# Image 0 of a convolution-and-attention kernel: its start in a written order, a place of its own for the rows of each unit, both halves' angles at once, image 1's statistics moved

## The chip, the cores and the metric

The kernel runs on one core of a Trainium2 chip. The core has five engines with queues of their own: PE (TensorE, matrix multiplication), DVE (VectorE), ACT (ScalarE), POOL (GpSimd) and SP (SyncE, which here issues every DMA). The metric is the device time of one execution in microseconds (us); shorter is better. All data is float32. PE writes to PSUM, which this kernel uses as six banks of 128 x 512 for general use and two for accumulators; everything else on the chip lies in SBUF, 128 partitions wide.

## What is computed

The input `x` is a batch of 16 images of 256 channels and 64 x 64 pixels. Two layers follow each other, each of the form x = x + layer(groupnorm(x)), where the group norm has 32 groups of 8 channels.

```python
# layer 0
pooled = x.mean(axis=(2, 3))
h = relu(pooled @ ap_w1.T + ap_b1)
angles = tanh(h @ ap_w2.T + ap_b2) * (pi / 4)
rot = vmap(vmap(_rotate_one))(base_kernel, angles)     # bilinear rotation of 3x3 kernels
out = conv(x, rot)                                      # 8 groups of 32 channels, own kernels per image
mod = sigmoid(relu(pooled @ meta_w1.T + meta_b1) @ meta_w2.T + meta_b2)
x = x + out * mod
# layer 1
q = xt @ Wq.T + bq;  k, v = split(xt @ Wkv.T + bkv)
scale = softplus(scale_param)
q, k = focused(relu(q) / scale), focused(relu(k) / scale)   # cubed, length kept
z = 1 / (q . k.sum + 1e-6)
out = q @ (k^T v) * z + depthwise5x5(v)
x = x + (out @ Wproj.T + bproj)
```

The statistics of the first norm need the whole image, so in each image the order is forced: statistics, angles and modulation, rotated kernels, convolution (with the residual folded in as an identity in the kernel's centre), statistics of the second norm, keys and values for all pixels, then queries and output.

## The kernel before

**Tiles.** An image is cut into 8 chunks (`NCH`) of 512 pixels; 256 channels are two halves of 128 partitions. `load_stats` loads a chunk into a buffer of the pool `xin` (12 buffers, tag "x"), `take_stats` has DVE take its statistics (`bn_stats`, one for each half). The convolution takes two chunks at a time, a **unit** `u` of four quarters `q` (a chunk and a half each); `load_rows` brings a unit's pixels, with one row above and one below, to 32 partitions per quarter in four DMAs. Where the row lies outside the image it is filled with the channel's mean (`edge`), by POOL.

**Preparation of an image.** `prepare(b)` is a generator; each `yield` ends a piece. In turn: group norm coefficients, the two small networks, tanh and sines, the `edge` values, then for each half `weights(t)` (angles to bilinear weights `mix`), `products` (POOL multiplies the base kernel by three of the nine mixes), `reduce` (DVE sums nine products), `finish`, `spread` (ACT copies the rotated kernels into the layout `wt` that PE reads), and `shifts` (48 small matmuls for both halves that give the bias which stands for the subtracted mean). For image 0 all pieces are written one after the other. For later images one piece is taken in each half of a `key_step` of the image before: for image 1 in the steps 4 to 15 of image 0, two pieces a step; what is left is taken in front of `between`. From image 2 on three pieces come earlier, at the end of the attention of the image before that.

**Convolution.** `convolve(b, u)` issues the unit's matmuls, 32 x 32 tiles on 16 places of PE at once, into four of the six PSUM banks. The first 16 products need all four quarters and all four `j` of `wt`. `evict` (ACT) moves a bank to SBUF and adds `shift`, `settle` (DVE) corrects the edge columns and takes the statistics of the second norm.

**Image 0.** Its units' rows go to two buffers in turn (`rows_of`: `xr`, and part of the tile `fm` that the attention uses later), so units 2 and 3 are loaded when the convolutions of units 0 and 1 have read theirs. Then `norm1(0)` gives the coefficients of the second norm, and the keys follow, 16 steps of 256 pixels. In the steps 0 to 3 the statistics of image 1 are taken, two chunks a step; `load_kernels(1)` and `prepare(1)` start at step 4.

**Order.** From the statement `with tc.manual_schedule()` in front of the image loop on, each engine works in the order in which the program is written. Everything in front of it (statistics of image 0, `prepare(0)`, the constants, the softplus of the scale and the scaling of `Wq` and `Wkv` by it, the zeros around `vpad`, four units of convolution) is ordered by a planner that may exchange independent instructions. Constants for the attention (`wp`, `band`, `dwb`, ...) are loaded by SP behind the first rows. `vh` holds the values in the layout of the 5 x 5 depthwise convolution; POOL sets it to zero once, and its margin columns stay zero for the whole run.

Of the kernel before, what the change touches and what calls it, by code (L numbers as in the profile page):

```python
# [15 lines left out]
P = 128  # L16
# [34 lines left out]
def conv_attention(ctx: ExitStack, tc: tile.TileContext, x, consts, kw, b1, w2, b2, b2r,  # L51
# [55 lines left out]

    for i in range(NCH):
        load_stats(0, i)
        take_stats(0, i)  # L110
# [21 lines left out]

    xbuf = [const("xr", [P, 4, CROWS])]
    xbuf.append(fmp.tile([P, 16, C], F32, tag="fm", name="xr_first").rearrange("p T n -> p (T n)")
                [:, 0:4 * CROWS].rearrange("p (g n) -> p g n", g=4))

    def rows_of(b, u):
        return xbuf[u % 2 if b == 0 else 0]
# [44 lines left out]
    def prepare(b):  # L183
# [5 lines left out]
        for t in range(2):  # L189
            nc.vector.tensor_scalar(gm[:, t, :], gmask, mean[:, t:t + 1], None, ALU.mult)  # L190
# [36 lines left out]
        state[b]["edge"] = edge  # L227
        nc.vector.tensor_scalar(mod, mod, 0.5, 0.5, ALU.mult, ALU.add)
# [8 lines left out]
        def weights(t):  # L237


            u = rotp.tile([P, 18], F32, tag="u", name=f"u_{b}_{t}")  # L240
            nc.vector.tensor_scalar(u, cgrid, cs[:, 0, t:t + 1], None, ALU.mult)
            nc.vector.scalar_tensor_tensor(u, sgrid, cs[:, 1, t:t + 1], u, ALU.mult, ALU.add)
            hat = rotp.tile([P, 3, 18], F32, tag="hat", name=f"hat_{b}_{t}")
            nc.vector.tensor_scalar(hat[:, 0, :], u, -1.0, 0.0, ALU.mult, ALU.max)
            nc.vector.tensor_scalar(hat[:, 2, :], u, 0.0, None, ALU.max)
            nc.vector.tensor_add(u, hat[:, 0, :], hat[:, 2, :])
            nc.vector.tensor_scalar(hat[:, 1, :], u, -1.0, 1.0, ALU.mult, ALU.add)
            yield
            mix = rotp.tile([P, 9, 9], F32, tag="mix", name=f"mix_{b}_{t}", bufs=2)
            hx = hat[:, :, 0:9].rearrange("p k n -> p n k")  # L250
            hy = hat[:, :, 9:18].rearrange("p k n -> p n k")
            nc.vector.tensor_scalar(hat[:, :, 9:18], hat[:, :, 9:18], a[:, t:t + 1], None, ALU.mult)
            nc.vector.tensor_mul(
                mix.rearrange("p n (y x) -> p n y x", y=3),
                hy.unsqueeze(3).to_broadcast([P, 9, 3, 3]),
                hx.unsqueeze(2).to_broadcast([P, 9, 3, 3]),
            )
            base = kw_t[:, ts(t, KB)].rearrange("p (o q) -> p o q", q=9)
            nc.gpsimd.tensor_mul(base, base, mod[:, t].unsqueeze(2).to_broadcast([P, HD, 9]))
            rots.append(rotp.tile([P, 9, HD], F32, tag="rotw", name=f"rot_{b}_{t}", bufs=2))  # L260
            mixes.append(mix)
            bases.append(base)
# [9 lines left out]

        def reduce(t, n, tmp):
            nc.vector.tensor_reduce(rots[t][:, 3 * n:3 * n + 3], tmp, AX.X, ALU.add)

        def finish(t):
            rs = rotp.tile([P, 3, HD], F32, tag="rsum", name=f"rsum_{b}_{t}")
            nc.vector.tensor_reduce(rs, rots[t].rearrange("p (r x) o -> p x o r", x=3), AX.X, ALU.add)
            sums.append(rs)

            nc.gpsimd.tensor_add(rots[t][:, 4], rots[t][:, 4], sel[:, 0:HD])
# [18 lines left out]
        yield from weights(0)  # L300
        yield
        for t in range(2):
            for n in range(3):
# [5 lines left out]
                if n == 0 and t == 0:  # L309
                    yield from weights(1)  # L310
# [5 lines left out]
                if t == 1 and n == 1:  # L316
                    shifts(0)
        for j in range(4):
            spread(1, (j,))
            yield  # L320
        shifts(1)

    def load_rows(b, u):


        for q in range(4):
            i, t = 2 * u + q // 2, q % 2
            src = x[b, ts(t, P)].rearrange("(g c) n -> c g n", g=4)
            lo, hi = CH * i - W, CH * (i + 1) + W
            d = rows_of(b, u)[ts(q, HD)]  # L330
            mean = state[b]["edge"][ts(q, HD), ts(t, 4)].unsqueeze(2).to_broadcast([HD, 4, W])
            if lo < 0:
                nc.gpsimd.tensor_copy(d[:, :, 0:W], mean)
                nc.sync.dma_start(d[:, :, W:CROWS], src[:, :, 0:hi])
            elif hi > N:
                nc.gpsimd.tensor_copy(d[:, :, CROWS - W:CROWS], mean)
                nc.sync.dma_start(d[:, :, 0:CROWS - W], src[:, :, lo:N])
            else:
                nc.sync.dma_start(d, src[:, :, lo:hi])
# [42 lines left out]
    for _ in prepare(0):  # L382
        pass
    for u in range(2):
        load_rows(0, u)

    wp_t = const("wp", [P, 2, C], halves(wp))
    bp_t = const("bp", [P, 2], bp)  # L390
    dwb_t = const("dwb", [P, 2], dwb)
    band_t = const("band", [KP, HD, BR * BC], band)
# [4 lines left out]
    for name, src, bsrc in (("kv", wkv, brow[C:3 * C]), ("q", wq, brow[0:C])):  # L397
# [6 lines left out]
    inv_t, sa, se, su = (  # L404
        wsp.tile([P, C], F32, tag=k, name=f"soft{n}") for n, k in enumerate(("wkv", "wq", "bkv", "bq"))
    )
    sw = rp.tile([P, C], F32, tag="r1", name="soft4")
    nc.sync.dma_start(inv_t, srow.partition_broadcast(P))


    nc.scalar.activation(sa, inv_t, AF.Abs)
    nc.scalar.activation(se, sa, AF.Exp, scale=-1.0)
    nc.vector.tensor_scalar(su, se, 1.0, None, ALU.add)
    nc.scalar.activation(sa, su, AF.Ln)
# [18 lines left out]

    pb = bank("pb")[:, 0:2]
    for co in range(2):
        for t in range(2):
            nc.tensor.matmul(pb[:, co:co + 1], lhsT=wp_t[:, t, ts(co, P)], rhs=dwb_t[:, t:t + 1],
                             start=t == 0, stop=t == 1)
    nc.vector.tensor_add(bp_t, bp_t, pb)


    vpad = [dcp.tile([BC, H + 4, NJ, C], F32, tag=f"vpad{n}", name=f"vpad{n}") for n in range(2)]
    zt = xp.tile([BC * NJ, 2, C], F32, tag="x", name="zero")
    nc.gpsimd.memset(zt, 0.0)
    for v in vpad:
        for k in range(BC):
            for y in (0, H + 2):
                nc.sync.dma_start(v[k, y:y + 2].rearrange("y j n -> j y n"), zt[0:NJ])


    vh = const("vh", [KP, NR // 2, NJ, C])
    nc.gpsimd.memset(vh, 0.0)


# [129 lines left out]
    def depthwise(b, half, c):  # L584
# [5 lines left out]
        vb = vh.rearrange("p R (m j) (c h) -> p R m j c h", j=4, h=NH)  # L590
# [114 lines left out]
    for u in range(NCH // 2):  # L705
        convolve(0, u)
        for q in range(4):
            evict(0, u, q)
            settle(0, u, q)
        if u < 2:  # L710
            load_rows(0, u + 2)
    fold_load(0, "kv")
    for _ in norm1(0):
        pass

# [67 lines left out]
    def attention_step(b, p, chain):  # L783
# [76 lines left out]
        if u and u < 3:  # L860
            load_rows(b + 1, u + 1)
# [11 lines left out]
    with tc.manual_schedule():  # L873
        fold_load(0, "q")
        made = iter(())
        for b in range(B):
            more = b + 1 < B
            state[b]["f"], state[b]["xq"] = {}, {}
            for n in range(0 if b == 0 else LEAD, NP):
                if b == 0 and n < 4:  # L880
                    load_stats(1, 2 * n)
                    load_stats(1, 2 * n + 1)
                if b == 0 and n == 4:
                    load_kernels(1)
                    made = prepare(1)
                key_step(b, n, made)
                if b == 0 and n < 4:
                    take_stats(1, 2 * n)
                    take_stats(1, 2 * n + 1)
# [11 lines left out]
                if more and n == 11:  # L901
                    load_rows(b + 1, 0)
# [93 lines left out]
```

## Time and profile before

| What | Value |
|---|---|
| Time, three runs | 3578.04, 3578.64 (median), 3583.35 us |
| Span of the profiled execution | 3572.8 us |
| PE busy (matmul) | 3457.5 us, 97% |
| PE weight loads | 2681.7 us, 75% |
| DVE, ACT, POOL busy | 66%, 56%, 45% |
| DMA | 514.58 MB, 144 GB/s in the mean |
| First 250 us: PE busy | 184.6 us |

The profile is of one execution; its span runs from the first to the last instruction, and the run times contain 5.8 us more than it in the median. A row of a table of windows gives the length, the busy time (and count) of PE, PE's weight loads, DVE, ACT and POOL, the clock granted to PE as a share of full speed, the busy share of the 16 DMA engines and GB/s. A row of the order of time gives start, duration, engine, line of the kernel, operation, output and inputs, and in brackets the idle time before it and what ended it. The clock record of this execution begins at 50.3 us; before that the column shows 1.00.

Statistics of image 0 end at 15.2 us, the copies of the rotated kernels run from 39.4 to 46.6, the four units of convolution end at 56.8, 66.8, 92.0 and 102.2, the keys start at 114.2 and the first unit of image 1 runs from 201.8 to 214.8.

### The profile page before, as it was taken

The page shows a single profiled execution, that of the slowest core. Times are in us where ns is not written, and L with a number is a line of the kernel's source. Part 1 is how long each engine was busy: PE and PEld are TensorE (multiplying, and loading weights), DVE is VectorE, ACT ScalarE, POOL GpSimd, SP SyncE. Part 2 cuts the span into 40 slices and gives each one's busy share as a digit, 9 for nine tenths or more (in the row PEclk, how much of TensorE's full clock was granted, in tenths as well). Part 3 has the DMA queues.
Part 4 walks back from the last instruction along what each step waited for, and adds up shares of the span by engine and source line. Part 5 has one row for each costly group of instructions (what it writes and reads, how often), then busy time and mean ns, then how long its engine had stood idle before and what let it go on. Part 6 is the DMA issues. An engine that isn't in the chain of part 4 may idle for free. (4 is left out here: it accounts for less than half of the span.)

```text
span 3572.8 us, 114570 instructions
## 1 busy us (share of the span) xinstructions
PE 3457.5 (97%) x46568; PEld 2681.7 (75%) x46568; DVE 2341.4 (66%) x6627; ACT 2010.2 (56%) x6501; POOL 1623.0 (45%) x1807
## 2 busy tenths in 40 slices
PE   4899999999999999999999999999999999999999
PEld 3577787777877768777786877878778787877878
DVE  4656667666685666756666676666756667566656
ACT  2454655647555565655646546474555656556465
POOL 3344545445353453534545344454544535345445
PEclk9999999999999999999999999999999999999999
DMA  6353552635546254452645526355363544625242
GB/s 182 109 161 115 156 175 100 194 97 176 153 131 183 87 172 148 156 168 81 188 127 162 169 86 193 117 159 176 107 195 97 168 149 149 179 85 170 92 153 96
DMA packets 219857, 514.58 MB, mean 144 GB/s; under 512 B 26645, under 2 KB 99863, under 8 KB 207044
## 3 DMA queue, kind: packets, MB, share of 16 engines
q1 hardware_dynamic: 219332, 507.26, 45.8%
q8 instruction: 368, 6.03, 0.7%
q14 instruction: 157, 1.29, 0.1%
HBM read 371.63 MB, written 135.53 MB: 142 GB/s over the span
## 5 line engine op out<-in xcount | busy, mean ns | idle before, releaser
L524 PE MATMUL pk<-wkv,x 128*128 128x512 f32 x2048 | 957.4, 614 | 0.0
L662 POOL TENSOR_TENSOR o<-o,fm 128x256 f32<-128x256 f32 x512 | 362.1, 728 | 993.0 <-DVE o L660 852.0
L524 PEld LDWEIGHTS pk<-wkv,x 128*128 128x128 f32 x2048 | 616.1, 311 | 203.7 <-issue 2.8
L355 PE MATMUL pc<-xr,wt 32*32 32x504 f32 (+1 forms) x17856 | 623.7, 599 | 15.9 <-DMA xr<-in_x 8.6
L355 PEld LDWEIGHTS pc<-xr,wt 32*32 32x32 f32 x17856 | 387.8, 104 | 217.4 <-issue 101.7
L680 PE MATMUL py<-oT,wp 128*128 128x256 f32 x2048 | 505.9, 390 | 0.9 <-ACT oT L672 0.7
L619 PE MATMUL pq<-wq,xq 128*128 128x256 f32 x2048 | 489.6, 382 | 0.0
L500 ACT ACTIVATE r_k<-rk 128x256 f32<-128x256 f32 x1024 | 416.2, 408 | 112.4 <-POOL rk L503 69.0
L500 ACT ACTIVATE r_q<-rq 128x256 f32<-128x256 f32 x1024 | 413.7, 408 | 79.9 <-DVE rq L494 50.2
L368 ACT ACTIVATE x<-pc,shift 128x512 f32<-128x512 f32 x256 | 165.4, 690 | 442.3 <-PE pc L355 442.3
L680 PEld LDWEIGHTS py<-oT,wp 128*128 128x128 f32 x2048 | 370.0, 190 | 50.9 <-issue 3.6
L619 PEld LDWEIGHTS pq<-wq,xq 128*128 128x128 f32 x2048 | 370.8, 191 | 42.6
L544 ACT ACTIVATE rk<-rk,s_k 128x256 f32<-128x256 f32 x512 | 231.5, 499 | 253.9 <-POOL s_k L512 253.9
L493 DVE TENSOR_TENSOR pq<-pq,bq 128x512 f32<-128x512 f32 x256 | 177.2, 692 | 297.5 <-PE pq L619 297.3
L672 ACT COPY oT<-po 128x512 f32<-128x512 f32 x256 | 149.8, 585 | 391.9 <-PE po L670 391.4
L503 POOL TENSOR_TENSOR rk<-r_k,rk 128x512 f32<-128x512 f32 x256 | 327.5, 1279 | 70.5 <-ACT r_k L500 69.1
L512 POOL TENSOR_TENSOR s_k<-s_k,phalf 128x2 f32<-128x2 f32 x256 | 176.8, 691 | 388.9 <-DVE s_k L509 379.1
L503 POOL TENSOR_TENSOR rq<-r_q,rq 128x512 f32<-128x512 f32 x256 | 327.0, 1277 | 29.9 <-issue 28.1
L512 POOL TENSOR_TENSOR s_q<-s_q,phalf 128x2 f32<-128x2 f32 x256 | 178.9, 699 | 325.2 <-DVE s_q L509 262.4
L493 DVE TENSOR_TENSOR pk<-pk,bkv 128x256 f32<-128x256 f32 x512 | 218.1, 426 | 135.3 <-PE pk L524 133.5
L378 DVE TENSOR_TENSOR x<-x,shift 128x16 f32<-128x16 f32 x256 | 67.9, 265 | 324.0 <-ACT x L368 324.0
L651 PE MATMUL pn<-kvx,qT 128*128 128x132 f32 x2048 | 273.2, 277 | 0.0
(128 smaller groups left out, 5226.8 us busy)
## 6 DMA issues: line engine op xcount, KB each, us to landing
vh<-vpad SPq DMA_DIRECT2D x256, 384.0 KB
vh<-vpad SPq DMA_DIRECT2D x256, 360.0 KB
vpad<-v SPq DMA_DIRECT2D x512, 128.0 KB
out<-x SPq DMA_DIRECT2D x128, 512.0 KB
xr<-in_x SPq DMA_DIRECT2D x186, 320.0 KB
xs<-in_x SPq DMA_DIRECT2D x224, 256.0 KB
xr<-in_x SPq DMA_DIRECT2D x62, 288.0 KB
xs<-in_x SPq DMA_DIRECT2D x16, 512.0 KB
```

The source lines that it names most:

```text
L355: nc.tensor.matmul(pcs[q].rearrange("p (r w) -> p r w", w=W)[ts(j, HD), :, to:to + n], lhsT=wt[ts(q, HD), j, k, :], rhs=g[ts(q, HD), j, r: ...
L368: nc.scalar.activation(state[b]["x"][i][:, t, :], state[b]["pc"][q], AF.Identity, bias=state[b]["shift"][:, t, 3:4])
L493: nc.vector.tensor_add(pm, pm, bias)
L500: nc.scalar.activation(f["r2"][:, j, :], f["r"][:, j, :], AF.Square, accum_out=f["s"][:, k, j:j + 1])
L503: nc.gpsimd.tensor_mul(f["r"], f["r2"], f["r"])
L512: nc.gpsimd.tensor_tensor(f["s"][:, 3, :], f["s"][:, 2, :], phalf, ALU.pow)
L524: nc.tensor.matmul(pm, lhsT=state[b]["x"][n // 2][:, t, T % BC:CH:BC], rhs=w[:, t, :], start=t == 0, stop=t == 1)
L544: nc.scalar.mul(f["r"][:, j, :], f["r"][:, j, :], f["s"][:, 3, j:j + 1])
L619: nc.tensor.matmul(pq[:, j, :], lhsT=xq[:, t, ts(j, P)], rhs=w[:, t, :], start=t == 0, stop=t == 1)
L651: nc.tensor.matmul(pn[:, :, 4 * hh:4 * hh + 4], lhsT=qT[:, hh, j, :], rhs=kvx[:, hh], start=True, stop=True)
L662: nc.gpsimd.tensor_add(o, o, fm[:, 2 * (m % NCH) + j, :])
L680: nc.tensor.matmul(py[:, co].rearrange("p y (J c) -> p J y c", c=BC), lhsT=wp_t[:, t, ts(co, P)], rhs=oT[:, t, :].rearrange("p (J y c) -> ...
```

## The change

- A manual schedule is entered ahead of the first instruction, so that image 0's start is in the written order, too. All eight statistics loads are written ahead of the `bn_stats`.
- `rows_of`: four places for the rows of image 0's four units, two of them in the first two planes of `vh` (which now has 128 partitions and is set to zero at the start). All four are loaded one after the other, ahead of the constants; the margin columns of these planes are set to zero again behind the convolutions. `load_rows` is split into the loads and `load_edges`; for image 0 the means are written by ACT.
- `angles()` replaces `weights(t)`: both halves in instructions of 36 elements. Both products of base kernel and modulation come ahead of it.
- Image 0's rotation is written out: five of the six products on POOL, the sixth on DVE as three `scalar_tensor_tensor` (`own_products`); the identity is added by DVE; half 1 is spread by DVE but for j = 3. Its `shifts` follow the matmuls of the first unit.
- For later images both `shifts` stand together, three pieces behind the last `spread`.
- The softplus' first four instructions and the load for it stand ahead of the rows and of `prepare(0)`; its addition of one is done by POOL. `wp`, `band` and the zeros of `vpad` follow the weights. The four matmuls for `bp` move behind the convolutions.
- Image 1's statistics: two chunks are loaded ahead of the constants, the others behind units 0 and 2; taken by DVE in the units 1, 2 and 3 (two chunks each), the last two behind `norm1(0)`. `load_kernels(1)` moves to key step 0 and `prepare(1)` starts at step 1.

```diff
+    ctx.enter_context(tc.manual_schedule())
     for i in range(NCH):
         load_stats(0, i)
+    for i in range(NCH):
         take_stats(0, i)
...
+    vh = const("vh", [P, NR // 2, NJ, C])
+    nc.gpsimd.memset(vh, 0.0)
...
+    for k in range(2):
+        xbuf.append(vh[:, k].rearrange("p J n -> p (J n)")[:, 0:4 * CROWS].rearrange("p (g n) -> p g n", g=4))
     def rows_of(b, u):
-        return xbuf[u % 2 if b == 0 else 0]
+        return xbuf[u if b == 0 else 0]
...
-        for t in range(2):
-            nc.vector.tensor_scalar(gm[:, t, :], gmask, mean[:, t:t + 1], None, ALU.mult)
+        nc.vector.tensor_mul(gm, gmask.unsqueeze(1).to_broadcast([P, 2, 4]), mean.unsqueeze(2).to_broadcast([P, 2, 4]))
...
         state[b]["edge"] = edge
+        if b == 0:
+            load_edges(0, 0)
...
+        def angles():
...
+            nc.vector.tensor_mul(u, grid(cgrid), part(0))
+            nc.vector.tensor_mul(w, grid(sgrid), part(1))
+            nc.vector.tensor_add(u, u, w)
+            hat = rotp.tile([P, 3, 2, 18], F32, tag="hat", name=f"hat_{b}")
+            nc.vector.tensor_scalar(hat[:, 0], u, -1.0, 0.0, ALU.mult, ALU.max)
+            nc.vector.tensor_scalar(hat[:, 2], u, 0.0, None, ALU.max)
+            nc.vector.tensor_add(u, hat[:, 0], hat[:, 2])
+            nc.vector.tensor_scalar(hat[:, 1], u, -1.0, 1.0, ALU.mult, ALU.add)
+            for t in range(2):
+                nc.vector.tensor_scalar(hat[:, :, t, 9:18], hat[:, :, t, 9:18], a[:, t:t + 1], None, ALU.mult)
             yield
+            for t in (1, 0):
+                mix = rotp.tile([P, 9, 9], F32, tag=f"mix{t}", name=f"mix_{b}_{t}")
+                nc.vector.tensor_mul(
...
+        for t in range(2):
             base = kw_t[:, ts(t, KB)].rearrange("p (o q) -> p o q", q=9)
             nc.gpsimd.tensor_mul(base, base, mod[:, t].unsqueeze(2).to_broadcast([P, HD, 9]))
...
+        def own_products(t, n):
+            tmp = xp.tile([P, 3, HD, 9], F32, tag="x", name=f"rtmp_{b}_{t}_{n}")
+            for k in range(3):
+                nc.vector.scalar_tensor_tensor(
+                    tmp[:, k], mixes[t][:, 3 * n + k, :].unsqueeze(1).to_broadcast([P, HD, 9]), 1.0, bases[t],
+                    ALU.mult, ALU.mult)
+            return tmp
...
-        yield from weights(0)
+        yield from angles()
         yield
+        if b == 0:
+            made = {k: products(*k) for k in ((0, 0), (0, 1), (0, 2), (1, 1), (1, 2))}
+            made[1, 0] = own_products(1, 0)
+            for t in range(2):
+                for n in range(3):
+                    reduce(t, n, made[t, n])
+                row_sums(t)
+                nc.vector.scalar_tensor_tensor(rots[t][:, 4], sel[:, 0:HD], 1.0, rots[t][:, 4], ALU.mult, ALU.add)
+                if t == 0:
+                    spread(0, range(4))
+            for j in range(3):
+                for q in (1, 3):
+                    nc.vector.tensor_copy(wt[ts(q, HD), j], rots[1][ts(j, HD)])
+            spread(1, (3,))
+            state[b]["late"] = shifts
+            return
...
-                if n == 0 and t == 0:
-                    yield from weights(1)
...
-                if t == 1 and n == 1:
-                    shifts(0)
...
+        for _ in range(3):
+            yield
+        shifts(0)
         shifts(1)
...
     load_kernels(0)
-    for _ in prepare(0):
-        pass
-    for u in range(2):
+    inv_t, sa, se, su = (
...
+    nc.sync.dma_start(inv_t, srow.partition_broadcast(P))
+    nc.scalar.activation(sa, inv_t, AF.Abs)
+    nc.scalar.activation(se, sa, AF.Exp, scale=-1.0)
+    nc.gpsimd.tensor_scalar(su, se, 1.0, None, ALU.add)
+    nc.scalar.activation(sa, su, AF.Ln)
+    for u in range(NCH // 2):
         load_rows(0, u)
+    for i in range(2):
+        load_stats(1, i)
...
     for u in range(NCH // 2):
         convolve(0, u)
+        if u == 0:
+            for t in range(2):
+                state[0]["late"](t)
+            load_edges(0, NCH // 2 - 1)
+            for i in range(2, 6):
+                load_stats(1, i)
+        else:
+            for i in {1: (0, 1), 2: (2, 3), 3: (4, 5)}[u]:
+                take_stats(1, i)
+                if u == 2:
+                    load_stats(1, i + 4)
         for q in range(4):
             evict(0, u, q)
             settle(0, u, q)
-        if u < 2:
-            load_rows(0, u + 2)
+    nc.gpsimd.memset(vh[:, 0:2, 0, :], 0.0)
+    nc.gpsimd.memset(vh[:, 0:2, NJ - 1, :], 0.0)
+    pb = bank("pb")[:, 0:2]
...
     fold_load(0, "kv")
     for _ in norm1(0):
         pass
+    for i in (6, 7):
+        take_stats(1, i)
...
-                if b == 0 and n < 4:
-                    load_stats(1, 2 * n)
-                    load_stats(1, 2 * n + 1)
-                if b == 0 and n == 4:
+                if b == 0 and n == 0:
                     load_kernels(1)
+                if b == 0 and n == 1:
                     made = prepare(1)
                 key_step(b, n, made)
-                if b == 0 and n < 4:
-                    take_stats(1, 2 * n)
-                    take_stats(1, 2 * n + 1)
```

## The prediction

> **What bounds the kernel.** I read the page first: PE is busy 97% of 3572.8 us, and the chain that ended last is almost all PE work. The stretches 250 to 1000, 1000 to 2000 and 2000 to 3000 us hold 11, 17 and 10 us without PE work; the first 250 hold 65, so only the start can pay. There I read the waits of PE:
>
> ```profile
> PE pm L161 <- DVE mv L155: 26.0, 3, 15.8
> PE pbias L294 <- DVE rsum L278: 14.6, 1, 14.6
> PE pc L355 <- DMA xr<-in_x: 8.6, 1, 8.6
> PE pbias L294 <- DVE s_k L508: 3.4, 1, 3.4
> ```
>
> (total us, times, longest). The reader is to see four places: image 0's statistics, its kernel rotation, rows that have not landed, and image 1's preparation that is not finished when its bias matmuls come up. Then the stages, each window's busy time by engine, granted clock, DMA share and GB/s:
>
> ```profile
> 43.40:56.80 13.40, 13.40 (x290) 8.42 (x295) 4.51 (x11) 6.90 (x14) 0.00 (x0) 1.00 0.19 45
> ...
> 66.80:75.40 8.60, 0.04 (x1) 0.00 (x0) 3.21 (x8) 2.23 (x4) 0.83 (x2) 0.75 0.93 208
> 75.40:92.00 16.60, 15.65 (x290) 7.06 (x292) 0.00 (x0) 0.00 (x0) 0.00 (x0) 0.72 0.91 226
> 92.00:102.20 10.20, 10.16 (x304) 6.29 (x284) 3.22 (x8) 2.69 (x5) 0.00 (x0) 1.00 0.01 3
> 102.20:114.20 12.00, 4.64 (x8) 2.52 (x9) 5.60 (x17) 2.15 (x4) 0.70 (x1) 0.62 0.01 1
> ...
> 133.10:138.50 5.40, 0.00 (x0) 0.00 (x0) 5.30 (x15) 3.07 (x12) 2.42 (x3) 0.76 0.19 65
> ...
> 193.90:201.80 7.90, 4.48 (x36) 3.31 (x32) 5.27 (x17) 6.07 (x21) 4.11 (x5) 0.72 0.27 85
> 201.80:214.80 13.00, 13.00 (x295) 8.23 (x298) 1.72 (x4) 7.73 (x25) 3.69 (x4) 0.78 0.10 35
> ```
>
> A unit of convolution takes 10.2 us when nothing is late (92.0 to 102.2). The third unit lies idle 8.6 us while DMA runs at 0.93, and then takes 16.6. At 133.1 PE is empty while DVE is full (5.30 of 5.40). The clock falls after each idle stretch: the convolution at 201.8 takes 13.0 us at 0.78, against 9.67 for the same 288 matmuls at 242.0. Last, the rows of the order of time that price the edits:
>
> ```profile
> 22.57 1.28 ACT L220 ACT_TABLE_LOAD   x1
> 23.87 0.29 ACT L220 ACTIVATE cs<-cs,pi 128x2 f32<-128x2 f32 x1
> ...
> 24.54 0.47 DVE L242 SCALAR_TENSOR_TENSOR u<-consts,cs,u 128x18 f32<-128x18 f32 x1
> ...
> 26.19 0.23 DVE L242 SCALAR_TENSOR_TENSOR u<-consts,cs,u 128x18 f32<-128x18 f32 x1
> 26.42 5.61 POOL L266 TENSOR_TENSOR rtmp<-mix,kw 128x864 f32<-128x864 f32 x3 [1.44 <-DVE u L242]
> ...
> 28.45 1.76 DVE L246 TENSOR_TENSOR u<-hat 128x18 f32<-128x18 f32 x1
> ...
> 39.43 7.15 ACT L286 COPY wt<-rot 32x288 f32<-32x288 f32 x16 [15.17 <-POOL rot L281]
> ...
> 119.60 2.46 DVE L106 BATCH_NORM_STATS2 st<-xs 128x6 f32<-128x512 f32 x4
> ```
>
> An 18-element DVE instruction lasts 1.76 us while POOL multiplies, and the same scalar_tensor_tensor 0.47 or 0.23 us with and without POOL beside it: a DVE instruction with two SBUF inputs waits for POOL's to end.
>
> **1. Rotation of image 0.** Statistics end at 15.2 us, since DVE is full with 16 x 0.67; the written order leaves that. The chain to the angles (24.2) keeps its instructions. Now the softplus stands before it on ACT (Abs, Exp, Ln: 3 x 0.42, and three table loads of 1.28 with Tanh's) and POOL (one add, 0.4 to 0.7 by its 32x256 copy and 128x256 add). Its source is queued behind kw, whose packets end at 16.0, so it lands near 16.3 and ACT is free for Tanh at 16.3 + 1.3 + 3.8 = 21.4, before the 22.2 at which Tanh starts now. Cover 0.8 us; a later landing delays everything one for one, POOL's power (18.1) included. I take 0, ends 0 and +5.
> The Trainium skill's "ScalarE: Activation LUTs", section "What ACT_TABLE_LOAD costs", speaks against this move: each switch is put at 1.28 us plus a drain, 2.66 in all. By the trace's row the activation starts 1.30 us after its load; by the page ACT would be free at 25.5 and Tanh 3.3 us late, which would make the total 3550.5.
> Angles: 16 DVE instructions become 11, but both halves are needed first. Nine dependent steps of 0.2 from 24.2 and two mixes of 0.24 end near 26.4, as half 0 does now (26.28). POOL then makes five products of 1.87 instead of six. The sixth is three scalar_tensor_tensor on DVE (0.41 by the 1x256 row, so 0.45 each), with two SBUF inputs: the first slips in, the others wait for POOL's ends, 28.4 and 30.6. So DVE starts reducing at 31.0: 3 x 1.05 and 0.48 end at 34.6, copies of half 0 run on ACT from 35 (8 x 0.45 to 38.6), the other three reductions, sum and add end at 38.8, and six copies on DVE (0.20 to 0.33 by the tensor_scalar rows of 64 and 256 elements) end at 40.5 beside two on ACT. Against 46.6 now (39.43 + 7.15). If DVE did not wait for POOL it would be 38.7; if POOL lost all of DVE's time, 43. I take 40.5.
>
> **2. First unit.** From 46.6 it ended at 56.8, having waited for weights and a low clock: 32 weight loads took 1.68 us until 50.3, then 1.07. For that clock it paid 1.4 (10.2, and 0.9 of work done before 46.6, less the full-clock 9.7); image 1's first unit paid 3.3 (13.0 - 9.7). I take 2.0: 40.5 + 9.7 + 2.0 = 52.2.
> The bias matmuls now come behind it: 48 in 2 x 0.61 us on PE, two more PSUM banks of six, and three DVE steps per half before ACT may evict. The next unit waits for banks: 1.2 to 4 us, I take 2.5. DVE must be free: the softplus tail and weight scaling (8.4 us, rows 52.9 to 61.2) run from 40.5 to about 49, if wlkv and wlq have landed. 16 row loads at 1.53 each (8 took 15.6 to 27.9) end near 41, two statistics chunks at 1.36 at 43.5, the weights at 46: margin 3.2. Second unit ends at 52.2 + 10.0 + 2.5 = 64.7, against 66.8.
>
> **3. Third and fourth unit.** All rows are in by 41. 35.4 us become 2 x 10.2 = 20.4: 85.1, against 102.2. Image 1's statistics (2 x 1.35 per unit) and settling (4 x 0.86) fill 6.1 of DVE's 10.2.
> SP's order costs something here: `band` (107 packets of 4096 B, one after another, 28.6 to 46.0) now starts near 46 and ends at 64. Zero fills behind it wait for it (they do now, 4.1 us), eight more take 6.6, the scaled weights 2.6; image 1's chunks 2 to 5 are issued at 74 to 79 and land by 80, when DVE wants them at 75 to 85. I charge 1.0 in the next part (0 to 4).
>
> **4. First norm, 102.2 to 114.2.** Same chain, 12.0, with 0.2 for the bias add and that 1.0. The eight small matmuls (1.9) and two POOL memsets hide behind settling (102.7 to 106.8). Keys start at 98.3.
>
> **5. Keys to the end of image 1's first convolution, 114.2 to 214.8 = 100.6 us.** Out go the 5.4 idle (four statistics groups of 2.46 in key steps of 4.9 us, where PE needs 3.6), half of 4.0 at the low clock after it, the 3.4 idle at 193.9 (30 advances now hold 29 pieces of preparation; there were 24 for 27), 2.0 of clock after that, and 13.0 - 9.7 = 3.3 in the convolution: 16.1. Two chunks (2.7 on DVE) come ahead of the first key bias; six banks of 1.8 us cover them, I add 0.6. If cover or preparation fails, half of the 16.1 stays. Result: 98.3 + 85.1 = 183.4, against 214.8: **31.4 us less**.
> The Trainium skill's "TensorE: Matmul & The Clock Gate", Part 1, puts the low state at half rate until a busy window of 3.4 us has passed. No run here shows what sets the window; by a page window and half rate the first unit would pay 1.7 instead of my 2.0, total 3546.9.
>
> **6. Other images.** 15 preparations lose six small DVE instructions each, off PE's path; the bias matmuls move to the last key step. I take 0, ends -0.3 and +0.5 us per image: -4 to +7.
>
> **Sum.** 3572.8 - 31.4 = 3541.4 of span. The runs' median is 5.8 above the profiled span; 3547.2 in all. Low end: rotation 1.8, clock 0.6, banks 1.3, queue 1.0, the last waits of part 5 1.8, other images 4 less: 3537. High end: rotation 2.5, clock 1.3, banks 1.5, queue 3, half of part 5 8, half of part 6 3.5 more: 3567.
>
> **Rivals.**
> *DVE stays the bound of the first key pass.* For: 6 x 0.42 + 0.3 per step, 13 us of preparation over 15 steps and waits of up to 0.99 behind POOL make some 4.2, PE's own 3.6 + 0.6. Against: 138.5 to 193.9 ran that load with 1.8 idle. Part 5 then gives 0: 3563. Chance 0.13.
> *The queue is later still.* If `wlkv` lands after 52 or chunks after 85, DVE stands in order behind them and settling, eviction and norm with it: 6 in unit 1, 6 in the norm: 3559. For: SP issues in order behind `band`. Chance 0.13.
> *Slower.* In every later image the bias matmuls take two of six banks immediately before the next image's convolution; if DVE is behind there, PE waits the 3.4 of the row above, the clock falls, and the convolution pays 3.3: 6.7 x 15 = 100, 3648. It decides from 2.2 us per image. Against: values, bias and query matmuls give DVE 4.3 us for 2.5 of work. Chance 0.05.
> *It does not do what it says.* If the row loads of units 2 and 3 wait for something late, part 3's 15 stay; with part 5 giving nothing either, its 16 stay too, and 3578 is no change. Chance 0.07, of it 0.05 within 0.2%, 0.01 on each side.
> *Forecast*, own range 3538 to 3556: 0.62.
>
> The 8-in-10 range is 3537 to 3567. About 0.2% (7 us) can be told from no change: below 3571.5 lie the forecast and the first two rivals: faster 0.62 + 0.13 + 0.13 + 0.01 = 0.89, same 0.05, slower 0.06.
>
> **What would show it.** Weight copies ended at 39 to 42 us; scalar_tensor_tensor rows near 1.9 us; no wait of the third unit on xr; convolutions ended near 85; key groups 4.2 us apart from the start; no clock dip before image 1's first convolution, which ends near 183; period of later images 216 to 219 as now. Wrong: a Tanh waiting behind Ln, DVE idle on wlkv or xs, PE gaps ahead of convolutions in later images.

## The result, and the profile after

| | Before | After |
|---|---|---|
| Median of six runs, us | 3582.27 (3578.04 to 3590.41) | 3652.15 (3636.04 to 3656.76) |
| Span of the profiled execution, us | 3572.8 | 3634.3 |
| Convolutions of image 0 end | 102.2 | 88.1 |
| Keys of image 0 start | 114.2 | 99.5 |
| First unit of image 1 | 201.8 to 214.8 | 171.4 to 181.1 |
| Last unit of an image to the first unit of the next, mean of 14 | 100.37 (100.1 to 100.6) | 106.66 (106.5 to 107.0) |
| First to last unit of an image, sum of 15 | 1760.3 | 1764.1 |
| Behind the last unit | 205.5 | 205.5 |

The ratio on record is 1.0172, 95% interval [1.0152, 1.0192]; the quotient of the two medians is 1.0195. So the kernel is slower by 1.7 to 2.0%, where 0.9% faster was forecast. The last four rows of the table are worked out from the starts and ends of PE's convolution instructions. They split the loss. The first unit of image 1 starts 30.4 us earlier; each of the 14 stretches behind it takes 6.29 us more, 88.1 together; the convolving stretches take 3.8 more; −30.4 + 88.1 + 3.8 = 61.5, which is the difference of the spans. So the start came about as forecast, and the loss lies where the forecast had put a zero. The profiled execution of the changed kernel (3636.04) is the fastest of its six; what the others lost beside it, 16 us in the median, stays unexplained.

First the windows of the start in the profile of the changed kernel (columns as before):

```profile
33.00:53.50 20.50, 15.99 (x289) 8.47 (x290) 17.79 (x34) 5.08 (x12) 5.81 (x4) 1.00 0.77 193
53.50:66.00 12.50, 12.50 (x340) 8.65 (x342) 6.44 (x18) 2.42 (x4) 0.00 (x0) 0.86 0.14 39
66.00:77.00 11.00, 11.00 (x322) 7.08 (x306) 4.52 (x10) 3.39 (x6) 0.00 (x0) 1.00 0.67 214
77.00:88.10 11.10, 10.07 (x277) 5.48 (x265) 6.78 (x14) 2.06 (x5) 0.00 (x0) 1.00 0.88 315
88.10:99.50 11.40, 5.64 (x17) 3.41 (x18) 5.47 (x18) 1.82 (x4) 1.69 (x3) 0.59 0.01 1
99.50:171.40 71.90, 71.79 (x639) 50.03 (x637) 59.83 (x174) 50.34 (x177) 43.07 (x42) 0.99 0.49 153
171.40:181.10 9.70, 9.70 (x297) 6.42 (x300) 1.72 (x4) 5.29 (x18) 3.90 (x4) 1.00 0.35 125
```

The third and fourth unit together take 22.1 us with no 8.6 us wait for rows (they overlap by some tenths, and 77.0 is not the exact border); the key pass of image 0 has PE busy for 71.79 of 71.90; the convolution at 171.4 runs in 9.7 at full clock. Now the waits of PE from 260 us on, first of the kernel before, then of the changed one (total us, times, longest; `pd` is the depthwise convolution):

```profile
PE pd L594 <- issue: 16.4, 19, 2.1
...
PE pkv L557 <- ACT rk L544: 0.4, 1, 0.4
```

```profile
PE pkv L592 <- ACT rk L579: 65.3, 37, 3.2
PE pd L629 <- issue: 21.0, 18, 2.1
```

One wait has appeared: the matmuls of keys and values (`pkv`) wait for the scaled keys `rk`, 65.3 us where there were 0.4. The clock record adds the rest: between 300 and 3300 us PE is at half clock 17 times for 3.4 us, in the kernel before once. Of the 17, 14 begin within 2 us of the end of a wait of `pkv`, one in each of the 14 stretches; the other three follow waits of `pd`, as does the one of the kernel before. If PE loses half of each entry, that is 14 × 3.4 × 0.5 = 24 us, and 24 + 65 = 89, against the 88.1 found above for the stretches. (The Trainium skill's "TensorE: Matmul & The Clock Gate", Part 1, gives a half rate and a window of 3.4 us; these entries agree with both.)

What holds up `rk` is seen in the order of time of the changed kernel, in the key steps of image 2, which carry the preparation of image 3 (start, duration, engine; in brackets idle time before and its releaser). In a key step POOL cubes a block of keys, ACT takes the sums of squares, DVE divides two such sums (the ratio), POOL takes a power of it (the root), and ACT scales the keys by that:

```profile
573.01 1.91 POOL L285 TENSOR_TENSOR rtmp<-mix,kw 128x864 f32<-128x864 f32 x1
573.09 0.42 ACT L535 ACTIVATE r_k<-rk 128x256 f32<-128x256 f32 x1 [0.34 <-POOL rk L538]
574.96 1.05 DVE L301 TENSOR_REDUCE rot<-rtmp 128x96 f32<-128x864 f32 x1 [1.72 <-POOL rtmp L285]
...
576.25 0.16 DVE L543 RECIPROCAL s_k<-s_k 128x2 f32<-128x2 f32 x1
576.44 0.16 DVE L544 TENSOR_TENSOR s_k<-s_k 128x2 f32<-128x2 f32 x1
...
576.68 0.69 POOL L547 TENSOR_TENSOR s_k<-s_k,phalf 128x2 f32<-128x2 f32 x1 [1.76 <-DVE s_k L544]
...
577.34 1.27 POOL L538 TENSOR_TENSOR rk<-r_k,rk 128x512 f32<-128x512 f32 x1
577.41 0.91 ACT L579 ACTIVATE rk<-rk,s_k 128x256 f32<-128x256 f32 x2 [2.61 <-POOL s_k L547]
...
578.58 1.92 POOL L285 TENSOR_TENSOR rtmp<-mix,kw 128x864 f32<-128x864 f32 x1
```

This is a ring: cube (L538, 1.27) on POOL, behind it in POOL's queue the product for the rotation (L285, 1.91), on DVE its reduction (L301, 1.05), behind that in DVE's queue the ratio (L543, L544, 2 × 0.16), on POOL the root (L547, 0.69), and the next cube. 1.27 + 1.91 + 1.05 + 0.32 + 0.69 = 5.24, and the next root starts at 581.93, 5.25 later. The ratio needs only ACT's squares, done at 574.0, 2.2 us earlier; it waits because the reduction stands in front of it and waits 1.72 for POOL.

The kernel before has such a step, too, but one only. POOL's roots (L512) and products (L266) there:

```profile
599.78 0.69 POOL L512 TENSOR_TENSOR s_k<-s_k,phalf 128x2 f32<-128x2 f32 x1 [3.23 <-DVE s_k L509]
...
601.67 1.92 POOL L266 TENSOR_TENSOR rtmp<-mix,kw 128x864 f32<-128x864 f32 x1
...
606.48 0.69 POOL L512 TENSOR_TENSOR s_k<-s_k,phalf 128x2 f32<-128x2 f32 x1 [2.90 <-DVE s_k L509]
...
609.01 1.92 POOL L266 TENSOR_TENSOR rtmp<-mix,kw 128x864 f32<-128x864 f32 x1
...
611.03 0.69 POOL L512 TENSOR_TENSOR s_k<-s_k,phalf 128x2 f32<-128x2 f32 x1
...
614.96 0.69 POOL L512 TENSOR_TENSOR s_k<-s_k,phalf 128x2 f32<-128x2 f32 x1
...
619.79 0.70 POOL L512 TENSOR_TENSOR s_k<-s_k,phalf 128x2 f32<-128x2 f32 x1
```

The first product costs a step of 6.70 (part of the angles of half 1 is in it, too); from the second on the steps are 4.55, 3.93 and 4.83. Between the two the code has the difference: `yield from weights(1)` behind the first reduction holds one `yield`. The two halves of a key step take one piece each, so that piece moves products two to six into the second half and their reductions into the first half of the next step, behind the ratio. `angles()` has no such piece, and all six products stay in the first half.

### The profile page after: what moved, and what is told of

Same layout as the page of the kernel before. It is cut to its first block, busy times and chain, and to the rows that moved or that the text cites. A ratio compares the mean times of both kernels' runs of the same rounds, so it can differ in the third digit from the quotient of the medians.

```text
span 3634.3 us, 114472 instructions
## 1 busy us (share of the span) xinstructions
PE 3475.8 (96%) x46568; PEld 2684.7 (74%) x46568; DVE 2289.3 (63%) x6541; ACT 2004.0 (55%) x6499; POOL 1619.8 (45%) x1803
## 3 DMA queue, kind: packets, MB, share of 16 engines
q14 instruction: 157, 1.29, 0.1%
## 5 line engine op out<-in xcount | busy, mean ns | idle before, releaser
L559 PE MATMUL pk<-wkv,x 128*128 128x512 f32 x2048 | 972.9, 623 | 0.0
L406 PE MATMUL pc<-xr,wt 32*32 32x504 f32 (+1 forms) x17568 | 607.4, 594 | 14.4 <-ACT wt L316 12.7
L535 ACT ACTIVATE r_q<-rq 128x256 f32<-128x256 f32 x1024 | 413.9, 408 | 81.7 <-DVE rq L529 52.4
L547 POOL TENSOR_TENSOR s_k<-s_k,phalf 128x2 f32<-128x2 f32 x256 | 176.9, 691 | 425.3 <-DVE s_k L544 419.2
L538 POOL TENSOR_TENSOR rk<-r_k,rk 128x512 f32<-128x512 f32 x256 | 327.1, 1278 | 57.2 <-ACT r_k L535 54.9
L538 POOL TENSOR_TENSOR rq<-r_q,rq 128x512 f32<-128x512 f32 x256 | 326.6, 1276 | 29.9 <-issue 29.9
L547 POOL TENSOR_TENSOR s_q<-s_q,phalf 128x2 f32<-128x2 f32 x256 | 179.1, 700 | 347.4 <-DVE s_q L544 318.2
L629 PE MATMUL pd<-vh,band 107*32 107x128 f32 x8192 | 243.8, 277 | 22.9 <-issue 22.6
```

What stands on the lines that cost most here:

```text
L406: nc.tensor.matmul(pcs[q].rearrange("p (r w) -> p r w", w=W)[ts(j, HD), :, to:to + n], lhsT=wt[ts(q, HD), j, k, :], rhs=g[ts(q, HD), j, r: ...
L535: nc.scalar.activation(f["r2"][:, j, :], f["r"][:, j, :], AF.Square, accum_out=f["s"][:, k, j:j + 1])
L538: nc.gpsimd.tensor_mul(f["r"], f["r2"], f["r"])
L547: nc.gpsimd.tensor_tensor(f["s"][:, 3, :], f["s"][:, 2, :], phalf, ALU.pow)
L559: nc.tensor.matmul(pm, lhsT=state[b]["x"][n // 2][:, t, T % BC:CH:BC], rhs=w[:, t, :], start=t == 0, stop=t == 1)
L629: nc.tensor.matmul(pd[ts(j, HD), k, :].rearrange("p (R m h) -> p R m h", R=4, m=4), lhsT=band_t[:, c + k, :], rhs=vb[:, :, :, j, c + k, :] ...
```

## The experiments

"Stretch" is from the last unit of an image to the first unit of the next, mean of 14, in the profiled execution. Every ratio is to the kernel before, run on the same chip, with its 95% interval.

### Which half of a key step

The changed kernel with one, then with two more pieces ahead of the products (the pieces at the end cut by as many):

```diff
         yield from angles()
         yield
+        if b >= 2:
+            yield
...
-        for _ in range(3):
+        for _ in range(2 if b >= 2 else 3):
             yield
```

> From image 2 on, one empty piece stands between the mixes and the first product, and one empty piece less stands before the bias matmuls, so these keep their place. Products move from the first half of a key step to the second, reductions from the second to the first. Theory (a loop: cube 1.28, product 1.91, reduction 1.05, ratio 0.35, root 0.69 and handovers, some 5.4 us a key step against PE's 4.2, because the reduction stands in front of the next step's ratio and the product in front of its root): the stretch from the last unit of an image to the first unit of the next falls from 106.6 to 100.3 us as before the change, total about 3540 of span, 88 to 95 us under the changed kernel, 0.99 of the kernel before. Rival (the bias matmuls and their two banks in the last key step): nothing changes, 106.6, ratio 1.017. Rival (nine DVE instructions of both halves in one piece): nothing changes either.

> Two empty pieces in place of one, two less before the bias matmuls: every product is a whole key step later, in the same half as in the changed kernel. Loop theory: as the changed kernel, 106 us from last to first unit, ratio 1.015 to 1.02. If it were only that products come too early in the pass, it would be faster than with one piece: 100, ratio 0.99.

One piece: 3544.1 us, ratio 0.9878 [0.9859, 0.9897], stretch 99.57; the wait of `pkv` is gone (0.4). Two pieces: 3620.33 us, ratio 1.0089 [1.0068, 1.0110], stretch 105.13, `pkv` waits 47.3. Not the number of pieces counts but whether it is odd or even: one more is fast, none and two more are slow. Two pieces lose somewhat less than none (105.13 against 106.66), and the ratio lies below the 1.015 to 1.02 expected; why was not looked into. With one piece the stretch is 0.8 us shorter than in the kernel before, which has one slow step of its own; by the steps above, such a step costs 0.8 (5.24 − 4.44).

Roots and products of the kernel with one piece more, in the same place:

```profile
573.55 1.92 POOL L285 TENSOR_TENSOR rtmp<-mix,kw 128x864 f32<-128x864 f32 x1
...
575.57 0.69 POOL L549 TENSOR_TENSOR s_k<-s_k,phalf 128x2 f32<-128x2 f32 x1
...
578.39 1.92 POOL L285 TENSOR_TENSOR rtmp<-mix,kw 128x864 f32<-128x864 f32 x1
...
580.40 0.70 POOL L549 TENSOR_TENSOR s_k<-s_k,phalf 128x2 f32<-128x2 f32 x1
...
584.33 0.69 POOL L549 TENSOR_TENSOR s_k<-s_k,phalf 128x2 f32<-128x2 f32 x1
```

Steps of 4.83 and 3.93, with no idle time ahead of a root.

The same from the other side: the kernel before with one piece more ahead of its angles, and the kernel before with `angles()` in place of `weights` and nothing else.

```diff
+        if b >= 2:
+            yield
         yield from weights(0)
```

```diff
-        yield from weights(0)
+        yield from angles()
...
-                if n == 0 and t == 0:
-                    yield from weights(1)
```

> The kernel before with one empty piece ahead of the angles from image 2 on, nothing else. Its first product then falls into the second half of a key step and the other five into the first half, with their reductions in the second. Loop theory: the loss of the changed kernel with five of six products, 100.4 us from last to first unit become 104.5 to 106, total 60 to 80 us more, ratio 1.016 to 1.022. If the loss needs the changed generator itself: 100.4 and ratio 1.00.

> The kernel before with the generator of both halves' angles alone: start, rows, statistics of image 1 and bias matmuls as before the change. One piece fewer lies between the first and the second product, so from image 2 on all six products fall into the first half. Loop theory: 106.6 us from last to first unit, 14 x 6.3 = 88 more, less up to 5 in image 1, whose products change to the second half: ratio 1.022 to 1.026. If fewer DVE instructions were what counts: ratio 0.999 or less. If the loss needs the bias matmuls' new place: ratio 1.00.

3641.16 us, ratio 1.0145 [1.0118, 1.0173], stretch 103.84; and 3676.05 us, ratio 1.0236 [1.0199, 1.0273], stretch 107.98. In the first of the two the first product moves into the good half while five move out of it, four steps net. The loss, 3.5 us a stretch, is about half as large and lies below the 104.5 to 106 expected: the waits of `pkv` here are 1.4 us at the longest, and only two half-clock entries follow one, where the changed kernel has 14. Four steps at 0.8 and 2 × 1.7 / 14 make 3.4. In the second the angles alone make the whole loss. They also do something for image 1. None of its pieces is taken ahead of the key steps, where three are for later images, so its products fall into the other half: in this kernel image 0's key pass (first key matmul to first unit of image 1) takes 78.2 us, 111.8 to 189.9, against 87.6 before. The first unit then takes 14.6 instead of 13.0, so 7.8 of the 9.4 remain. Whether the halves do this, or the one piece less, was not tried apart.

The forecast's slow case, bias matmuls that take two PSUM banks ahead of the next convolution, was tried by putting `shifts` back where it was:

```diff
+                if t == 1 and n == 1:
+                    shifts(0)
...
-        for _ in range(3):
-            yield
-        shifts(0)
         shifts(1)
```

> For later images the bias matmuls of half 0 go back behind the second product of half 1 and those of half 1 directly behind the last copy, as before the change; the three empty pieces go. Rival (bias matmuls and their banks, my slow case): 100 us from last to first unit, ratio 0.99. Loop theory: products and reductions keep their halves, so 106 to 107 us, ratio 1.015 to 1.02.

3653.95 us, ratio 1.0172 [1.0145, 1.0200], stretch 107.92, `pkv` waits 60.5: nothing comes back. That case falls, although its 3648 was near the time measured.

### Is it the ring

If the ring is what costs, it can be cut at another place: ratio and root of a step are issued at the end of the step before, ahead of the reduction, with the products left in the first half. (`between`, which issued them for the last steps, leaves out what is then already done; not shown.)

```diff
-        if n >= 2:
+        if n >= 2 and (b == 0 or n == LEAD):
             ratio(k[n - 2], False)
             root(k[n - 2])
...
+        if b > 0:
+            ratio(k[n - 1], False)
+            root(k[n - 1])
         next(made, None)
```

> All pieces stay where the changed kernel has them; from image 1 on ratio and root of a key step are issued at the end of the step before, in front of the piece with the reduction, instead of at its own beginning. Loop theory: the reduction no longer delays the ratio, POOL's own work is 1.28 + 1.91 + 0.69 = 3.9 us a step, under PE's 4.2, so the stretch falls to 100 to 102 us, ratio 0.99 to 0.995. If the product's place on POOL alone makes the loss (it still stands in front of the root): 104 to 106.6, ratio 1.01 to 1.017. Rival with the bias matmuls: 106.6.

3540.27 us, ratio 0.9865 [0.9850, 0.9880], stretch 99.64. The stretch is shorter than the 100 to 102 expected, and DVE and POOL do the same work, so the amount of their work was not the limit. Then both mends at once, and, after their result, two pieces more with the ratio ahead:

> The changed kernel with one piece later and the ratio and root of a key step ahead, together. Theory (either mend alone already takes the loop of cube, product, reduction, ratio and root below PE's own time per key step, so that PE is the bound of the stretch): stretch from the last unit of an image to the first of the next 99.3 to 99.8 us as with either alone (99.57 and 99.64), ratio to the kernel before 0.985 to 0.989. Rival (part of the loop still stands in PE's way after each mend): stretch below 99, 14 times 0.6 or more, ratio 0.984 or less.

> The changed kernel with two pieces later and the ratio and root of a key step ahead: the products are in the first half of a step again, between cube and root, where the root of the mend that was fast (ratio ahead alone) found them. Theory (the place of POOL's product in the ring of cube, squares, ratio, root decides, and both mends together were slow because the product of 1.92 us then stood between root and next cube, serial with the squares): fast, stretch from the last unit to the first 99.4 to 100.2 us, ratio to the kernel before 0.985 to 0.990. Rival (taking pieces later is itself what costs, since what is left of the preparation at the end of the steps grows): slow like two pieces later alone and both mends, stretch 104 to 106, ratio 1.005 to 1.011.

Both mends: 3620.91 us, ratio 1.0083 [1.0063, 1.0103], stretch 105.89. Neither theory had this; two cures together are the illness again. The order of time of that kernel shows why:

```profile
574.75 0.69 POOL L549 TENSOR_TENSOR s_k<-s_k,phalf 128x2 f32<-128x2 f32 x1 [1.48 <-DVE s_k L546]
...
575.40 1.95 POOL L285 TENSOR_TENSOR rtmp<-mix,kw 128x864 f32<-128x864 f32 x1
...
577.30 1.27 POOL L540 TENSOR_TENSOR rk<-r_k,rk 128x512 f32<-128x512 f32 x1
...
578.61 0.42 ACT L537 ACTIVATE r_k<-rk 128x256 f32<-128x256 f32 x1 [2.23 <-POOL rk L540]
...
579.55 0.17 DVE L545 RECIPROCAL s_k<-s_k 128x2 f32<-128x2 f32 x1
...
579.99 0.69 POOL L549 TENSOR_TENSOR s_k<-s_k,phalf 128x2 f32<-128x2 f32 x1 [1.41 <-DVE s_k L546]
```

The root now ends a step, and the product, in the second half, stands directly behind it on POOL, ahead of the next cube. Root 0.69, product 1.95, cube 1.27, then ACT's squares until the ratio can start at 579.55, 0.44 to the next root: 5.24 from root to root, a ring of the same length through ACT. In the kernel with the ratio ahead alone, the product stands between cube and root, and POOL multiplies while ACT squares; the ratio comes before the reduction:

```profile
577.47 1.92 POOL L285 TENSOR_TENSOR rtmp<-mix,kw 128x864 f32<-128x864 f32 x1
577.55 0.42 ACT L535 ACTIVATE r_k<-rk 128x256 f32<-128x256 f32 x1 [0.37 <-POOL rk L538]
...
578.49 0.17 DVE L543 RECIPROCAL s_k<-s_k 128x2 f32<-128x2 f32 x1 [0.30 <-ACT r_k L535]
...
579.43 1.05 DVE L301 TENSOR_REDUCE rot<-rtmp 128x96 f32<-128x864 f32 x1
579.49 0.70 POOL L547 TENSOR_TENSOR s_k<-s_k,phalf 128x2 f32<-128x2 f32 x1
```

That reading was put to the test by the last of the three: two pieces more put the product back into the first half. 3547.56 us, ratio 0.9876 [0.9859, 0.9892], stretch 99.60. Fast, as the ring has it; the four combinations are: second half with the ratio in its old place fast, first half with it slow, second half with the ratio ahead slow, first half with it fast.

### What the start gained, and from what

Three kernels with one piece more (3544.1) each undo a part of the start. Softplus behind the sines instead of ahead of everything:

```diff
-    nc.scalar.activation(sa, inv_t, AF.Abs)
-    nc.scalar.activation(se, sa, AF.Exp, scale=-1.0)
-    nc.gpsimd.tensor_scalar(su, se, 1.0, None, ALU.add)
-    nc.scalar.activation(sa, su, AF.Ln)
...
             load_edges(0, 0)
+            soften()
...
+    nc.vector.tensor_scalar(su, se, 1.0, None, ALU.add)
     nc.vector.tensor_scalar(su, su, -1.0, None, ALU.add)
```

(`soften()` is the three activations, Ln with a bias of 1; the zero fill's memset moves behind the preparation.)

> On top of one piece later: ACT's three softplus instructions stand behind the sines and the edge copies (the addition of one inside Ln's bias), DVE adds one later, and the zeros for the margins are made behind the rotation. Theory: the changed kernel's power on POOL waited 1.9 us behind the softplus' addition and the zeros, so the copies of the rotated kernels end at 40.4 to 41 instead of 42.6 and all that follows is 1.5 to 2 us earlier; total 2 us less, 0.987 of the kernel before. Rival (the wait was covered): nothing moves.

3545.92 us, ratio 0.9885 [0.9858, 0.9911]. The trace shows the power on POOL (L178) at 18.25 instead of 19.76 and the copies of the rotated kernels ended at 40.44 instead of 41.90; image 1's first unit starts at 169.8 instead of 171.3. So the softplus and the zero fill ahead of the power cost 1.5 us together, which the time can't tell.

Image 1's statistics back in the key steps 0 to 3, its preparation from step 4 (their loads and statistics in the units go; not shown):

```diff
-                if b == 0 and n == 0:
-                    load_kernels(1)
-                if b == 0 and n == 1:
+                if b == 0 and n < 4:
+                    load_stats(1, 2 * n)
+                    load_stats(1, 2 * n + 1)
+                if b == 0 and n == 4:
+                    load_kernels(1)
                     made = prepare(1)
                 key_step(b, n, made)
+                if b == 0 and n < 4:
+                    take_stats(1, 2 * n)
+                    take_stats(1, 2 * n + 1)
```

> On top of one piece later: image 1's statistics are loaded and taken in the key steps 0 to 3 again, and its kernels and preparation start at step 4, as before the change. Theory: DVE fills key steps of 4.9 us again and PE runs empty once, with a low clock behind it; the first unit of image 1 moves from 171.3 to 179 to 184 us and the total rises by 8 to 13, ratio 0.990 to 0.992. Rival (the statistics were hidden behind PE's six banks): 171 to 174.

3560.85 us, ratio 0.9922 [0.9897, 0.9947]. The wait that the kernel before had at 133.1 is back, in the waits of PE between 99 and 200 us:

```profile
PE pm L168 <- DVE mv L162: 5.4, 1, 5.4
PE pd L629 <- issue: 1.6, 1, 1.6
```

Image 1's first unit starts at 177.0, 5.7 later (179 to 184 was expected), and takes 14.4 instead of 9.7: 10.4 us. It starts before its last weights are copied, and PE waits 0.8 for them in it. The key pass takes 78.2, the same as in the kernel with the angles alone.

Two places for the rows again, units 2 and 3 loaded behind units 0 and 1 (`load_edges` for the last unit moves with them; not shown):

```diff
-        return xbuf[u if b == 0 else 0]
+        return xbuf[u % 2 if b == 0 else 0]
...
-    for u in range(NCH // 2):
+    for u in range(2):
         load_rows(0, u)
...
+        if u < 2:
+            load_rows(0, u + 2)
```

> The changed kernel with one piece later, but the rows of image 0 in two places again: units 2 and 3 are loaded behind the matmuls of units 0 and 1. Theory (a place of its own for each unit is what took the 8.6 us wait on xr and the 16.6 us unit away): image 0's convolutions end at 100 to 104 us instead of 87.9, all of it on the path since the stages of image 0 follow one another; first unit of image 1 at 183 to 187 instead of 171.3; time 12 to 16 us over the kernel with one piece later (3544.1), ratio to the kernel before 0.991 to 0.993. Rival (by then the DMA queue is free, since the order of the loads alone did it): convolutions end by 91, ratio 0.987 to 0.989.

3565.23 us, ratio 0.9919 [0.9898, 0.9939]. The third unit waits for rows and then runs while they arrive (its windows, 65.2 to 73.4 and 73.4 to 87.0):

```profile
65.20:73.40 8.20, 2.27 (x60) 0.82 (x60) 4.28 (x10) 3.33 (x6) 0.00 (x0) 0.94 1.08 249
73.40:87.00 13.60, 13.60 (x231) 6.20 (x232) 1.31 (x3) 0.00 (x0) 0.00 (x0) 0.66 0.92 247
```

Convolutions end at 98.8 instead of 87.9 and image 1 starts at 181.9 instead of 171.3: 10.6 us, where at least 12 was expected. The total lies further off, and it can't be used for the start: the convolving stretches of images 1 to 15, which none of these three edits touches, take 1781.3, 1780.4 and 1781.8 us in the three profiled executions, 13 to 14 more than with one piece more (1767.5). Why is open. So the start's worth is read from the positions here.

## Why the prediction was wrong, point by point

**Part 6, "Other images", is the step that failed.** It reads "15 preparations lose six small DVE instructions each, off PE's path … I take 0", with ends of −0.3 and +0.5 us per image. Measured: 6.29 us a stretch, 14 of them. It counted instructions, and what changed was the count of pieces: the `yield` inside `weights(1)` disappeared with it, products two to six and their reductions changed halves, and the reduction came to stand ahead of the ratio in DVE's queue. Both halves of the price stood in the trace of before: a step with the product in the first half, 6.70 between two roots, and the steps with it in the second, 4.55 and 3.93. Five steps that go from 4.44 (606.48 to 619.79 in three) to 5.24 give 4.0 us, and one half-clock entry a stretch 1.7 more: 5.7, where 6.3 was measured. Only the pieces of image 1 had been counted.

**Part 1, rotation.** Copies ended at 42.60 instead of 40.5, and the softplus and the zero fill ahead, taken at 0, are most of it (1.5 by the experiment). `srow` landed at 18.24, not 16.3, and the cost came by POOL's queue, not by ACT's tables. Here are the rows of the changed kernel:

```profile
18.24 0.42 ACT L440 ACTIVATE soft<-soft 128x256 f32<-128x256 f32 x1 [16.23 <-DMA soft<-in_srow]
...
19.12 1.28 ACT L443 ACT_TABLE_LOAD   x1
19.19 0.86 POOL L442 TENSOR_SCALAR soft<-soft 128x256 f32<-128x256 f32 x1 [4.35 <-ACT soft L441]
19.99 0.52 POOL L465 MEMSET zero<- 16x512 f32 x1
20.41 0.42 ACT L443 ACTIVATE soft<-soft 128x256 f32<-128x256 f32 x1
20.48 0.71 POOL L178 TENSOR_TENSOR co<-vs,mhalf 128x2 f32<-128x2 f32 x1
...
28.72 4.61 DVE L295 SCALAR_TENSOR_TENSOR rtmp<-mix,kw 128x288 f32<-128x288 f32 x3
28.91 9.90 POOL L285 TENSOR_TENSOR rtmp<-mix,kw 128x864 f32<-128x864 f32 x5 [2.37 <-issue]
```

The power waits behind the softplus' addition and a memset until 20.48 (18.1 before). The mixes end at 28.8 instead of 26.4, and from there to the last copy it took 13.8, where 14.1 was forecast: the three own products took 4.61 beside POOL; the forecast had them end 4.6 behind the mixes (26.4 to 31.0), because they wait for POOL. (Two SBUF inputs, by which the prediction told the DVE instructions that wait, do not set them apart in the kernel before: L244 and L247 there, with one, lasted 1.88 and 1.81 beside POOL's products.) As for the table loads, the load at 19.12 lasts 1.28 and Ln starts at 20.41, 1.29 behind the load's start; the 2.66 of the Trainium skill's "ScalarE: Activation LUTs", "What ACT_TABLE_LOAD costs", is not seen here.

**Parts 2 to 4.** First unit ended at 53.5 (52.2), second at 66.0 (64.7): the 12.5 between them is the 12.5 forecast, but by luck: 2.5 of it had been put down to waiting for banks, and PE is busy all the time. In place of that stand 0.98 for the bias matmuls and 12.5 × 0.14 = 1.75 for a clock of 0.86. Third and fourth together 22.1 instead of 20.4, with 1.03 us idle in the fourth. The first norm took 11.4 instead of 13.2. The rows' own places are worth 10.6 by the experiment; part 3 had put the two units at 15.0.

**Part 5.** Keys to the end of image 1's first unit: 81.6, where 85.1 was forecast and 100.6 stood before. The sum was nearly right and its grounds incomplete. It gave the whole to the statistics' place and the earlier start of the preparation. Over the same stretch, the kernel with the statistics back in the key steps takes 92.6 against 81.7 with one piece more, so those two give 10.9 together; and the angles alone, with the preparation still starting at step 4, take the kernel before from 100.6 to 92.8, another 7.8. The edit that ruined images 2 to 15 is the one that did this for image 1. Start in all: 33.7 gained (214.8 to 181.1), 31.4 forecast.

**The rivals.** "DVE stays the bound of the first key pass" falls: PE is busy for 71.79 of 71.90. "The queue is later still" falls: PE waits neither for `wlkv` nor for the chunks in the units, and the norm is shorter. DVE did stand idle for chunks, 5.4 us until 75.7 and 1.4 until 78.4, a sign that the prediction had named; they landed before the 85 of the rival, and PE stood idle for 1.03 us only. "It does not do what it says" falls with the third unit. "Slower" had the sign and, by chance, the size; its mechanism was not found in the trace, and taking it away changed nothing.

## What to carry to other kernels

When a generator's pieces are dealt out between the instructions of another stage, count the pieces before and after an edit, and write down for each engine's queue what each piece now stands in front of; one piece more or less can close a ring across engines that are far from full (here DVE 63% and POOL 45% busy). The version that beats both kernels is the changed one with the ratio ahead (3540.27 us, 1.35% faster, [0.9850, 0.9880]); one piece more alone is level with it within the intervals. Two mends of one ring are to be tried singly before they are combined.

## What the runs showed beyond that

A ring that leaves PE idle for 65.3 / 37 = 1.8 us at a time cost more than the idle time: each of the 14 stretches has one half-clock entry of 3.4 us that begins within 2 us of the end of such a wait, some 1.7 us of the 6.3. Eight of the 14 follow a single wait of 1.9 us; the kernel before with one piece more has 29 waits of 1.4 us at most, and two of them are followed by an entry. That two rings through different engines have the same length, 5.25 us by DVE's reduction and ratio and 5.24 by ACT's squares and the ratio, is by chance of their middle parts; root, cube and product on POOL, 3.9 us, are serial in both.
